# The first stage's silu by tanh, and softplus logarithms for two chunks at a time

## The chip, the cores and the metric

The kernel runs on one core of one Trainium2 chip. The metric is the device time of one execution in microseconds (us). Five engines work side by side, each through a queue of its own in order: PE (matmul, with its weight loads PEld), DVE (vector), ACT (activation functions), POOL (GpSimd) and SP, which here issues most DMAs. [...]

## The reference

The program takes `x` of 8 sequences x 512 positions x 256 channels, in fp32, through two blocks. The change touches the first alone. There, `xn = layernorm(x)` goes into a state-space branch and an FP4 feed-forward branch, and both are added to `x`:

```python
# state-space branch (d_inner 512, d_state 16)
x_in, z = split(xn @ W_in.T)                # 512 channels each
u = silu(causal_conv4(x_in, conv_w) + conv_b)
delta_raw, B, C = split(u @ W_xproj.T)      # 16, 16, 16
delta = softplus(delta_raw @ W_dt.T + b_dt)
h[t] = exp(delta[t] * A) * h[t-1] + (delta[t] * u[t]) * B[t]     # A = -exp(A_log), 512 x 16 states
y[t] = sum_n h[t] * C[t] + D_param * u[t]
attn = (y * silu(z)) @ W_out.T
# feed-forward branch (inner 704); fq: quantize to FP4 in blocks of 16 and back
ffn = fq(silu(fq(xn) @ fq(w_gate).T) * (fq(xn) @ fq(w_up).T)) @ fq(w_down).T
x = x + attn + ffn
```

The second block (block-sparse attention and a two-layer local-attention network) follows on the result, and is the same in both kernels.

## The kernel before, in words

The first stage keeps one sequence of 512 positions at a time on chip, channels on the 128 partitions. Three generators per sequence `b` write its work:

- `head(b)`: layernorm, transposes (`xt`), then for each of four chunks of 128 channels the input projection (`ps_in`), the convolution on DVE (L268, L272), and Silu on ACT into `u` (L275). Then `ps_xp`, and per chunk softplus: `ps_dt` on PE (L294), Abs and Relu (L297, L298), Exp (L299), two DVE operations (L300, L301), Ln (L302), three POOL operations (L303 to L305) that leave `delta` and `du` = delta x u. Softplus is computed as relu(v) + log(1 + exp(-|v|)), and the two DVE operations carry the rounding error of 1 + e.
- `scan(b)`: for two chunks at a time and each of 16 states, `bb` (B spread over the partitions, PE, L366), the product with `du` on DVE (L369), `da` = exp(delta x A) on ACT into PSUM (L374), the scan on DVE (L376), the product with C on POOL (L377), and the sum over states on PE (`y`, L378). After each pair of chunks: `ps_z` (L384), Silu into `z` (L389), the D term on DVE (L390) and the product with `z` on POOL (L393). At the end `ps_o` (L399), the sum into `xs` (L403), and a DMA of the result from ACT's queue (L404).
- `ffn(b)`: FP4 of `xn`, then for four tiles of 128 positions, in two halves of 352 columns: gate and up matmuls (`ps_g` L330, `ps_u` L336), Silu into `h` (L340), the product with up on DVE (L341); FP4 of `h`, transposes and `ps_d` (L350). `fp4` works on DVE (L96 to L100), POOL (L101), ACT (L105), DVE (L106 to L108) and POOL (L109).

`fp4_weights` does the same to the three FFN weights once. `evac` copies from PSUM, in turn on DVE (L50) and ACT (L52).

`beside(scan(b), chain(ffn(b), head(b + 1)), 34, 24)` (36 for the first sequence) interleaves the generators by counts of their `yield`s: while the scan's 34 steps go by, 24 steps of the others are written. A scheduler of the framework then orders each engine's queue from this program, so the order on an engine can differ from the text; it also puts in the table loads (ACT_TABLE_LOAD) that an ACT operation needs when its function isn't in the active table.

The pool `pmm` (tag "mm") has two PSUM banks, which nearly all matmuls of `head` and `ffn` and `ps_z`, `ps_o` share in turn; `bb` and `da` have two banks each, the two `y` one each. `rot` tiles have three buffers by tag (`cv` and `e` use "t0", `w` and `z` "t1"), `hh` six; `delta`, `du` and `u` have two, one for the sequence being scanned and one for the next.

Of the kernel before, what the change touches and what calls it, by code (L numbers as in the profile page):

```python
# [9 lines left out]
FP = mybir.dt.float32  # L10
BF = mybir.dt.bfloat16
AF = mybir.ActivationFunctionType
ALU = mybir.AluOpType
# [4 lines left out]
P = 128  # L18
NB, L, D = 8, 512, 256
NT = L // P  # L20
KC = D // P
DI, NS, DR = 512, 16, 16
NC = DI // P
# [15 lines left out]
def tile_kernel(ctx: ExitStack, tc: tile.TileContext, a: dict, out: bass.AP):  # L39
# [105 lines left out]
    with ExitStack() as s0:  # L145
# [25 lines left out]
        act.activation(a_neg, a_neg, AF.Exp)  # L171
        dve.tensor_scalar(a_neg, a_neg, -1.0, None, ALU.mult)


        sel = w0.tile([DR + 2 * NS, NS, P], FP, name="sel")
        for n in range(NS):
# [21 lines left out]
        def fp4_weights():  # L198
            for name, dst in (("w_gate", w_g), ("w_up", w_u)):
                src = a[name].rearrange("(j p) d -> p j d", p=FB)  # L200
                for j in range(0, FI // FB, 2):
                    raw = q.tile([P, FI], FP, tag="q_src", name="q_src")[:FB, : 2 * D]
                    act.dma_start(raw.rearrange("p (j d) -> p j d", j=2), src[:, j : j + 2, :])
                    fp4(raw, raw, FB, 2 * D, q, sm)
                    ps = pmm.tile([P, L], FP, tag="mm", name="ps_w")
                    for k in range(KC):
                        for i in range(2):
                            pe.transpose(
                                ps[:, (2 * k + i) * FB : (2 * k + i + 1) * FB],
                                raw[:, i * D + k * P : i * D + (k + 1) * P],  # L210
                                ident[:FB, :FB],
                            )
                    evac(
                        dst[:, :, j * FB : (j + 2) * FB],
                        ps[:, : 4 * FB].rearrange("p (k n) -> p k n", k=KC),
                    )
                    yield
            for r in range(D // P):
                raw = q.tile([P, FI], FP, tag="q_src", name="q_src")
                act.dma_start(raw, a["w_down"][r * P : (r + 1) * P, :])  # L220
                fp4(raw, raw, P, FI, q, sm)
                inner_to_partitions(raw, w_d[:, :, r * P : (r + 1) * P])
                yield
# [27 lines left out]
        def head(b):  # L251
            x = load_x(b)
            xn = w1.tile([P, NT, D], FP, tag="xn", name="xn")
            layernorm(x, xn, sm)
            xt = w1.tile([P, KC, L], FP, tag="xt", name="xt")
            to_channels(xn, xt, pmm, "mm")
            yield


            u = w1.tile([P, NC, L], FP, tag="u", name="u")  # L260
            for c in range(NC):
                ps = pmm.tile([P, L], FP, tag="mm", name="ps_in")
                for k in range(KC):
                    pe.matmul(
                        ps, w_in[:, k, c * P : (c + 1) * P], xt[:, k, :], start=(k == 0), stop=(k == KC - 1)
                    )
                cv = rot.tile([P, L], FP, tag="t0", name="cv")
                dve.tensor_scalar(  # L268
                    cv, ps, conv_w[:, c, 3:4], conv_b[:, c : c + 1], ALU.mult, ALU.add
                )  # L270
                for s in range(1, 4):
                    dve.scalar_tensor_tensor(  # L272
                        cv[:, s:], ps[:, : L - s], conv_w[:, c, 3 - s : 4 - s], cv[:, s:], ALU.mult, ALU.add
                    )
                act.activation(u[:, c, :], cv, AF.Silu)  # L275
                yield
            ps = pmm.tile([P, L], FP, tag="mm", name="ps_xp")
            for c in range(NC):
                pe.matmul(
                    ps[: DR + 2 * NS, :], w_xp[:, c, :], u[:, c, :], start=(c == 0), stop=(c == NC - 1)  # L280
                )
            xd = w1.tile([DR + 2 * NS, L], FP, tag="xd", name="xd")
            act.copy(xd, ps[: DR + 2 * NS, :])
            c_d = dram.tile([NS, L], FP, tag="c_d", name="c_d")
            sp.dma_start(c_d, xd[DR + NS :, :])
            yield

            delta = w1.tile([P, NC, L], FP, tag="delta", name="delta")  # L290
            du = w1.tile([P, NC, L], FP, tag="du", name="du")
            for c in range(NC):
                ps = pmm.tile([P, L], FP, tag="mm", name="ps_dt")
                pe.matmul(ps, w_dt[:, c * P : (c + 1) * P], xd[:DR, :], start=True, stop=True)  # L294
                e = rot.tile([P, L], FP, tag="t0", name="e")
                w = rot.tile([P, L], FP, tag="t1", name="w")
                act.activation(e, ps, AF.Abs, bias=b_dt[:, c : c + 1])  # L297
                act.activation(delta[:, c, :], ps, AF.Relu, bias=b_dt[:, c : c + 1])  # L298
                act.activation(e, e, AF.Exp, scale=-1.0)  # L299
                dve.tensor_scalar(w, e, 1.0, None, ALU.add)  # L300
                dve.scalar_tensor_tensor(e, w, 1.0, e, ALU.subtract, ALU.subtract)  # L301
                act.activation(w, w, AF.Ln)  # L302
                pool.tensor_tensor(w, w, e, ALU.subtract)  # L303
                pool.tensor_tensor(delta[:, c, :], delta[:, c, :], w, ALU.add)
                pool.tensor_tensor(du[:, c, :], delta[:, c, :], u[:, c, :], ALU.mult)  # L305
                yield
            made[b] = x, xn, xt, u, xd, c_d, delta, du

        def ffn(b):

            x, xn = made[b][:2]
            xs = sums[b] = w1.tile([P, NT, D], FP, tag="xs", name="xs")
            xq = one.tile([P, NT, D], FP, tag="xq", name="xq")
            for t in range(0, NT, 2):
                fp4(
                    xn[:, t : t + 2, :].rearrange("p t d -> p (t d)"),
                    xq[:, t : t + 2, :].rearrange("p t d -> p (t d)"),
                    P, 2 * D, q, sm,
                )
                yield  # L320
            xqt = one.tile([P, KC, L], FP, tag="xqt", name="xqt")
            to_channels(xq, xqt, pmm, "mm")
            for t in range(NT):
                h = q.tile([P, FI], FP, tag="q_src", name="h")
                n = FI // 2
                for half in range(2):
                    cols = slice(half * n, (half + 1) * n)
                    pg = pmm.tile([P, L], FP, tag="mm", name="ps_g")
                    for k in range(KC):
                        pe.matmul(  # L330
                            pg[:, :n], xqt[:, k, t * P : (t + 1) * P], w_g[:, k, cols],
                            start=(k == 0), stop=(k == KC - 1),
                        )
                    pu = pmm.tile([P, L], FP, tag="mm", name="ps_u")
                    for k in range(KC):
                        pe.matmul(  # L336
                            pu[:, :n], xqt[:, k, t * P : (t + 1) * P], w_u[:, k, cols],
                            start=(k == 0), stop=(k == KC - 1),
                        )
                    act.activation(h[:, cols], pg[:, :n], AF.Silu)  # L340
                    dve.tensor_tensor(h[:, cols], h[:, cols], pu[:, :n], ALU.mult)  # L341
                yield
                fp4(h, h, P, FI, q, sm)
                yield
                ht = q.tile([P, NI, P], FP, tag="ht", name="ht")
                inner_to_partitions(h, ht)
                ps = pmm.tile([P, L], FP, tag="mm", name="ps_d")
                for c in range(NI):
                    m = min(P, FI - c * P)
                    pe.matmul(  # L350
                        ps[:, :D], ht[:m, c, :], w_d[:m, c, :], start=(c == 0), stop=(c == NI - 1)
                    )
                dve.tensor_tensor(xs[:, t, :], x[:, t, :], ps[:, :D], ALU.add)
                yield

        def scan(b):

            x, xn, xt, u, xd, c_d, delta, du = made[b]
            for c0 in range(0, NC, 2):
# [20 lines left out]
                for i in range(2):  # L380
# [5 lines left out]
                            start=(k == 0), stop=(k == KC - 1),  # L386
                        )
                    z = rot.tile([P, L], FP, tag="t1", name="z")
                    act.activation(z, ps, AF.Silu)  # L389
                    dve.scalar_tensor_tensor(  # L390
                        u[:, c, :], u[:, c, :], d_par[:, c : c + 1], ys[i], ALU.mult, ALU.add
                    )
# [16 lines left out]
        for b in range(NB):  # L409
            rest = [ffn(b)] + ([head(b + 1)] if b + 1 < NB else [])  # L410
            if b == 0:
                rest = [fp4_weights(), *rest, rotary_tables()]
            beside(scan(b), chain(*rest), 34, 24 if b else 36)


    with ExitStack() as s1:
# [608 lines left out]
```

## Time and profile before

| | |
|---|---|
| three runs | 4056.45, 4067.31, 4068.78 us; median 4067.31 |
| the profiled execution | 4060.3 us, span 4058.3 us |
| the first stage's last output leaves (L404) | 1726.5 us after the span's start |
| busy share of the whole span | PE 91%, DVE 65%, ACT 42%, POOL 33% |
| mean granted PE clock | 0.91 of full speed |
| sequences leave the first stage (L404) | 313.4, 520.8, 728.6, 933.7, 1141.6, 1346.3, 1551.6, 1726.5 us |
| ACT_TABLE_LOAD in all | 297: 264 in the first stage, 33 in the second |

The page gives busy time by engine, and the span in 40 slices of 101.5 us with the busy share of each in tenths. A group's line has the source line, engine, operation, tiles and shapes, the count, then busy us and mean ns of one, then the engine's idle time just before it and what ended it. A line of the waits names the instruction that waited, what it waited for, and us in total, times and the longest. In an answer by stretch, each row has the length of the stretch, then each engine's busy time (with its count of rows in the trace).

### The profile page before, as it was taken

Reading aid. Unit: us, or ns where it says so; the run is one execution under the profiler, and the core shown is the slowest. Engines: PE = TensorE matmul, PEld = TensorE weight load, DVE = VectorE, ACT = ScalarE, POOL = GpSimd, SP = SyncE. Lnnn points to the kernel's source line nnn. Section 1 sums busy time; section 2 is a strip of 40 time slices with the busy share of each in tenths; the row PEclk is TensorE's granted clock in tenths of the full one; section 3 lists DMA queues with packets and bytes.
Section 4 is the critical chain, followed back from the end, with each engine's and each line's share of the span. In section 5 each row is a group of like instructions: output and inputs, shape, how many; then the busy total and the mean of one; then the engine's idle time right before and its main releaser. Section 6 shows DMA issues by size and latency. Waiting matters only on the chain.

```text
span 4058.3 us, 41394 instructions
## 1 busy us (share of the span) xinstructions
PE 3690.3 (91%) x14428; PEld 1757.7 (43%) x14444; DVE 2647.0 (65%) x4809; ACT 1724.7 (42%) x3411; POOL 1326.4 (33%) x1059
## 2 busy tenths in 40 slices
PE   5889898898988988989999999999999999999998
PEld 1334343434343434344553554544544445445545
DVE  7877879787978787765654555555455456456444
ACT  3454646455645555433343243244234234333333
POOL 4555556555655555521012012021111101201210
PEclk7788789888988888989999999999989999999999
DMA  2111111111111111120011011011101111100100
GB/s 84 45 39 47 45 47 50 44 47 44 47 47 46 49 39 47 60 88 27 27 53 42 14 56 43 20 45 43 38 27 43 38 40 34 53 27 27 48 27 6
DMA packets 88712, 171.96 MB, mean 42 GB/s; under 512 B 10024, under 2 KB 41768, under 8 KB 88504
## 3 DMA queue, kind: packets, MB, share of 16 engines
q1 hardware_dynamic: 85568, 162.95, 12.5%
q10 hardware_dynamic: 2936, 6.36, 0.4%
q8 instruction: 115, 1.88, 0.2%
q14 instruction: 93, 0.76, 0.1%
HBM read 159.58 MB, written 9.70 MB: 42 GB/s over the span
## 4 chain that ended last, share of the span: by engine, by line
PE 46%; DVE 7%; issue 2%; ACT 2%; POOL 1%; DMA 0%; SPq 0%; POOLq 0%; DVEq 0%; ACTq 0%
PE ps_qkv L707 8%; PE ps_g L877 5%; PE ps_a L877 4%; PE ps_wo L839 3%; PE ps_qk L538 3%; PE ps_y L912 2%; PE ps_w L895 2%; PE ps_st L633 2%; PE lo L811 2%; PE pt_qk L698 2%; PE ps_ls L759 2%; DVE pr L788 2%; PE pt L797 1%; DVE nm L769 1%; PE ps_s L583 1%
## 5 line engine op out<-in xcount | busy, mean ns | idle before, releaser
L377 POOL TENSOR_TENSOR hh<-hh,cb 128x512 f32<-128x512 f32 x512 | 660.3, 1302 | 452.3 <-PE y L378 116.8
L378 PE MATMUL y<-hh,ident 128*128 128x512 f32 x1024 | 640.5, 740 | 126.3 <-POOL hh L377 123.5
L376 DVE TENSOR_TENSOR_SCAN hh<-da,hh 128x512 f32<-128x512 f32 x512 | 604.9, 1206 | 11.2 <-ACT da L374 11.1
L374 ACT ACTIVATE da<-delta,a_neg 128x512 f32<-128x512 f32 x512 | 348.7, 689 | 441.1 <-DVE hh L376 439.6
L378 PEld LDWEIGHTS y<-hh,ident 128*128 128x128 f32 x1024 | 202.5, 223 | 460.1 <-POOL hh L377 341.7
L369 DVE TENSOR_TENSOR hh<-du,bb 128x512 f32<-128x512 f32 x512 | 333.9, 672 | 71.7 <-PE bb L366 63.1
L366 PE MATMUL bb<-xd,sel 48*128 48x512 f32 x512 | 311.0, 710 | 26.6 <-DVE hh L369 26.6
L775 ACT ACTIVATE pr<-ps_ls,nm 128x256 f32<-128x256 f32 (+1 forms) x512 | 221.8, 446 | 174.9 <-DVE nm L769 174.7
L726 POOL TENSOR_TENSOR r<-r,r 128x512 f32<-128x512 f32 x128 | 162.8, 1272 | 355.4 <-DVE r L724 355.4
L884 DVE SCALAR_TENSOR_TENSOR ht<-ps_a,b,gl 128x512 f32<-128x512 f32 x96 | 71.9, 749 | 252.1 <-PE ps_a L877 252.1
L487 POOL MEMSET sa<- 128x1 f32 x16 | 1.6, 102 | 711.9 <-DVE sa L843 384.6
L722 DVE TENSOR_TENSOR r<-ps_qkv,tab 128x512 f32<-128x512 f32 x128 | 87.9, 687 | 222.1 <-ACT sq L721 222.1
L883 ACT ACTIVATE gl<-ps_g,b 128x512 f32<-128x512 f32 x96 | 65.9, 686 | 379.4 <-PE ps_g L877 379.4
L877 PE MATMUL ps_g<-hn,wf 128*128 128x512 f32 (+1 forms) x384 | 207.6, 659 | 20.5 <-issue 20.4
L721 ACT ACTIVATE sq<-ps_qkv 128x512 f32<-128x512 f32 x128 | 76.6, 598 | 272.9 <-PE ps_qkv L707 272.9
L877 PE MATMUL ps_a<-hn,wf 128*128 128x512 f32 (+1 forms) x384 | 191.2, 618 | 0.0
L366 PEld LDWEIGHTS bb<-xd,sel 48*128 48x128 f32 x512 | 89.5, 207 | 234.6 <-DVE hh L369 94.6
L637 ACT ACTIVATE pt_e<-ps_st 128x512 f32<-128x512 f32 (+1 forms) x384 | 172.8, 536 | 14.6 <-PE ps_st L631 13.8
L769 DVE TENSOR_REDUCE nm<-ps_ls 128x2 f32<-128x512 f32 (+1 forms) x256 | 147.4, 617 | 43.4 <-PE ps_ls L759 42.6
L707 PE MATMUL ps_qkv<-wqkv,s 128*128 128x512 f32 x384 | 174.9, 605 | 0.0
L707 PE MATMUL ps_qkv<-wqkv,sf 128*128 128x512 f32 x384 | 173.3, 601 | 0.0
L788 DVE TENSOR_SCALAR pr<-pr,lrs 128x256 f32<-128x256 f32 (+1 forms) x512 | 148.6, 332 | 4.8
(213 smaller groups left out, 6622.1 us busy)
## 6 DMA issues: line engine op xcount, KB each, us to landing
cb<-c_d SPq DMA_DIRECT2D x256, 256.0 KB, 3.1
wqkv<-in_wqkv SPq DMA_DIRECT2D x16, 1536.0 KB, 6.2
wf<-in_wf SPq DMA_DIRECT2D x16, 1364.0 KB, 11.0
wf<-in_wf SPq DMA_DIRECT2D x16, 768.0 KB, 4.7
tab<-tab SPq DMA_DIRECT2D x18, 512.0 KB, 6.9
wo<-in_wo SPq DMA_DIRECT2D x16, 512.0 KB, 3.9
x<-in_x SPq DMA_DIRECT2D x8, 512.0 KB, 4.0
x<-xs ACTq DMA_DIRECT2D x8, 512.0 KB, 2.8
```

Source lines behind the costliest of these rows:

```text
L366: pe.matmul(bb, sel[:, n, :], xd, start=True, stop=True)
L369: dve.tensor_tensor(hs[i], du[:, c0 + i, :], bb, ALU.mult)
L374: act.activation(da, delta[:, c, :], AF.Exp, scale=a_neg[:, c, n : n + 1])
L376: dve.tensor_tensor_scan(hh, da, hh, 0.0, ALU.mult, ALU.add)
L377: pool.tensor_tensor(hh, hh, cb, ALU.mult)
L378: pe.matmul(ys[i], ident, hh, start=(n == 0), stop=(n == NS - 1))
L637: act.activation(pt[:, :n], banks[g][:, :n], AF.Exp)
L707: pe.matmul(ps, shifted(s, k, t * P, P), wqkv[:, k, i * IN : (i + 1) * IN], start=(k == 0), stop=(k == KC - 1),)
L769: dve.tensor_reduce(nm, banks[r][:, : 2 * nk].rearrange("p (g n) -> p g n", g=2), AX.X, ALU.max, negate=True)
L775: act.activation(pr[:, at], banks[r][:, at], AF.Exp, bias=nm[:, i : i + 1], accum_out=rs[:, i : i + 1],)
L788: dve.tensor_scalar(pr[:, at], pr[:, at], rs[:, i : i + 1], None, ALU.mult)
L877: pe.matmul(dst[:m], wf1[:, k, off + c * P : off + c * P + m], hn[:, k, :], start=(k == 0), stop=(k == KC - 1),)
```

## The change

Silu(v) is computed as (1 + tanh(v/2)) v/2. The halves are put into the weights once: `conv_w` and `conv_b`, the `z` half of `w_in` (DVE, at the start), and `w_g` (in the evacuation of the quantized gate weight, which moves from `evac` to ACT, with that of `w_u`). ACT writes tanh, and a new DVE operation forms (tanh + 1) times the halved argument: for `u` from SBUF, for the gate and `z` from the PSUM bank that the matmul wrote.

In softplus, `e` becomes one tile of four chunks with a single buffer, and `du` takes the place of `w`. Chunks go in pairs: both chunks' Abs, Relu, Exp and DVE operations first, then one Ln over both, then the POOL operations of both. A pair of chunks now yields four times where it yielded twice, so `head` has 14 steps, before 10, and `ffn` 14 as before; the last argument of `beside` goes from 24 to 28, and from 36 to 40 for the first sequence.

```diff
+        for t in (conv_w, conv_b, w_in[:, :, DI:]):
+            dve.tensor_scalar(t, t, 0.5, None, ALU.mult)
...
-                    evac(
-                        dst[:, :, j * FB : (j + 2) * FB],
-                        ps[:, : 4 * FB].rearrange("p (k n) -> p k n", k=KC),
+                    act.activation(
+                        dst[:, :, j * FB : (j + 2) * FB], ps[:, : 4 * FB].rearrange("p (k n) -> p k n", k=KC),
+                        AF.Copy, scale=0.5 if dst is w_g else 1.0,
                     )
...
-                act.activation(u[:, c, :], cv, AF.Silu)
+                act.activation(u[:, c, :], cv, AF.Tanh)
+                dve.scalar_tensor_tensor(u[:, c, :], u[:, c, :], 1.0, cv, ALU.add, ALU.mult)
...
-            for c in range(NC):
-                ps = pmm.tile([P, L], FP, tag="mm", name="ps_dt")
-                pe.matmul(ps, w_dt[:, c * P : (c + 1) * P], xd[:DR, :], start=True, stop=True)
-                e = rot.tile([P, L], FP, tag="t0", name="e")
-                w = rot.tile([P, L], FP, tag="t1", name="w")
-                act.activation(e, ps, AF.Abs, bias=b_dt[:, c : c + 1])
-                act.activation(delta[:, c, :], ps, AF.Relu, bias=b_dt[:, c : c + 1])
-                act.activation(e, e, AF.Exp, scale=-1.0)
-                dve.tensor_scalar(w, e, 1.0, None, ALU.add)
-                dve.scalar_tensor_tensor(e, w, 1.0, e, ALU.subtract, ALU.subtract)
-                act.activation(w, w, AF.Ln)
-                pool.tensor_tensor(w, w, e, ALU.subtract)
-                pool.tensor_tensor(delta[:, c, :], delta[:, c, :], w, ALU.add)
-                pool.tensor_tensor(du[:, c, :], delta[:, c, :], u[:, c, :], ALU.mult)
-                yield
+            e = one.tile([P, NC, L], FP, tag="e", name="e")
+            for c0 in range(0, NC, 2):
+                cs = (c0, c0 + 1)
+                for c in cs:
+                    ps = pmm.tile([P, L], FP, tag="mm", name="ps_dt")
+                    pe.matmul(ps, w_dt[:, c * P : (c + 1) * P], xd[:DR, :], start=True, stop=True)
+                    act.activation(e[:, c, :], ps, AF.Abs, bias=b_dt[:, c : c + 1])
+                    act.activation(delta[:, c, :], ps, AF.Relu, bias=b_dt[:, c : c + 1])
+                    act.activation(e[:, c, :], e[:, c, :], AF.Exp, scale=-1.0)
+                    dve.tensor_scalar(du[:, c, :], e[:, c, :], 1.0, None, ALU.add)
+                    dve.scalar_tensor_tensor(
+                        e[:, c, :], du[:, c, :], 1.0, e[:, c, :], ALU.subtract, ALU.subtract
+                    )
+                    yield
+                act.activation(du[:, c0 : c0 + 2, :], du[:, c0 : c0 + 2, :], AF.Ln)
+                for c in cs:
+                    w = du[:, c, :]
+                    pool.tensor_tensor(w, w, e[:, c, :], ALU.subtract)
+                    pool.tensor_tensor(delta[:, c, :], delta[:, c, :], w, ALU.add)
+                    pool.tensor_tensor(w, delta[:, c, :], u[:, c, :], ALU.mult)
+                    yield
...
-                    act.activation(h[:, cols], pg[:, :n], AF.Silu)
+                    act.activation(h[:, cols], pg[:, :n], AF.Tanh)
+                    dve.scalar_tensor_tensor(h[:, cols], h[:, cols], 1.0, pg[:, :n], ALU.add, ALU.mult)
...
-                    act.activation(z, ps, AF.Silu)
+                    act.activation(z, ps, AF.Tanh)
+                    dve.scalar_tensor_tensor(z, z, 1.0, ps, ALU.add, ALU.mult)
...
-            beside(scan(b), chain(*rest), 34, 24 if b else 36)
+            beside(scan(b), chain(*rest), 34, 28 if b else 40)
```

## The prediction

> **What bounds the kernel now.** I read the page's slices first, then busy time by stretch, then the groups of table loads, then the Vector engine's waits. The profiled execution has a span of 4058.3 us inside a time of 4060.3, 7.0 below the median of 4067.3; all sums below are made against 4060.3, and a difference is carried over to the median unchanged. The last output of the first stage leaves at 1726.5 us, so the stage is the first 17 of the 40 slices:
>
> ```profile
> PE   5889898898988988989999999999999999999998
> DVE  7877879787978787765654555555455456456444
> ACT  3454646455645555433343243244234234333333
> POOL 4555556555655555521012012021111101201210
> ```
>
> DVE and PE are both at 7 to 9 tenths in those slices, ACT at 3 to 6. ACT is where the change removes work, DVE is where it adds some. Busy time by stretch, cut where each sequence's result is sent to DRAM (columns: length, then PE, PEld, DVE, ACT, POOL busy, PE clock, DMA share, GB/s), shows the sixth, seventh and eighth of eight:
>
> ```profile
> 1141.60:1346.30 204.70, 181.69 (x420) 76.22 (x419) 163.77 (x229) 107.88 (x142) 115.47 (x91) 0.87 0.15 46
> 1346.30:1551.60 205.30, 180.35 (x424) 76.64 (x423) 168.50 (x226) 115.36 (x148) 118.37 (x92) 0.88 0.17 44
> 1551.60:1726.50 174.90, 158.81 (x379) 67.55 (x377) 132.95 (x177) 78.81 (x103) 93.79 (x75) 0.89 0.18 58
> ```
>
> The last stretch has no `head` of a next sequence beside it. It is 30 us shorter, and DVE is busy 33 us less (133.0 against a mean of 166.1). DVE's idle time is 41, 37 and 42 us, the same, although this stretch holds 21 table loads and the two before it 67, 33.5 each. That is the reading that I lean on: **DVE work passes into the stage's time nearly one for one, and fewer table loads alone don't shrink DVE's idle time.** It isn't clean: PE is busy 22 us less too and is the fuller engine there, so PE and DVE share the bound.
>
> The loads, from the groups of the first stage (line, count, busy us, mean ns, idle before):
>
> ```profile
> L374 ACT ACT_TABLE_LOAD x107 | 137.3, 1283 | 1.9
> L340 ACT ACT_TABLE_LOAD x57 | 73.1, 1283 | 1.0
> L302 ACT ACT_TABLE_LOAD x31 | 39.8, 1283 | 0.5
> ```
>
> With L389 (24), L275 (23), L299 (14), L56 (7) and L105 (1) they are 264, 264 x 1.283 = 339 us. What they cost DVE, from its waits in the stage (us in total, times, longest):
>
> ```profile
> DVE h L341 <- ACT h L340: 80.6, 34, 3.3
> DVE hh L369 <- PE bb L366: 63.1, 48, 4.2
> DVE w L300 <- ACT e L299: 26.4, 15, 6.0
> DVE h L341 <- PE ps_u L336: 22.2, 15, 2.5
> DVE q_m L106 <- ACT q_m L105: 16.7, 16, 3.5
> DVE hh L376 <- ACT da L374: 11.1, 10, 3.5
> ```
>
> With two small rows (4.0 and 0.5) ACT ends 139 us of DVE's waits. That, and not 339, is about what the loads can give back. ACT itself waits 440 us for the scan (`da` L374 for `hh` L376): most loads lie in slack.
>
> [...] the load at 946.68 us is followed by its `da` at 947.98, 1.30 later. [...] the trace agrees that Abs and Relu (L297, L298) load nothing, and has no tanh. [...] here a scalar_tensor_tensor takes 738 ns with a PSUM input (L390, 708 to 749) and 959 without (L301, 658 to 1633)[...].
>
> **The change, part by part.**
>
> *Table loads.* The order of the built program holds 42 loads in this stage: 16 before Ln, 16 back to exp (14 at `da`, 2 at the Exp of `e`), and the square roots with the way back. 222 x 1.283 = 285 us leave ACT. The Tanh that replaces Silu I take at Silu's durations (463 ns at 352, 597 to 630 at 512). Sixteen Ln of 1024 replace 32 of 512: fixed part about 0.2 us by the rows at 352 and 512, so 3 us less. All on ACT, so its worth is only what DVE, PE or POOL regain below.
>
> *New DVE work.* Gate of the FFN: 64 of 128x352 from PSUM, 516 (L341) + 50 for the scalar form (738 against 687 ns) = 0.57 us: 36.5. `z`: 32 at 0.738: 23.6. `u`: 32 with SBUF operands alone, 0.74 to 0.96, taken 0.85: 27.2. Scaling w_in, conv_w, conv_b: about 1.9. Four evacuations of gate and up weights go to ACT: -2.1. Together 87; neighbours overlap by some 0.07 us (two L369 in 1.27), 128 x 0.07 = 9 less: **+78**. The one-off scaling waits for w_in, which lands 6.3 us after 0.7, when DVE still has idle time.
>
> *FFN waits.* Now Silu of half 0 frees the gate's PSUM bank on ACT; after, the new DVE operation frees it, and the "mm" ring has two banks. In 23 of 32 tiles the built order puts gate, up, gate, up next to one another on DVE, so half 1 waits: matmuls 1.45 us (L330 at 1004.11), Tanh 0.46, less the 0.52 of the up product between: 1.4; with 0.3 around it 1.7 a tile, 54 in all, against 104 now (80.6 + 22.2 + 1.4). **-50**; from -85 (PE early) to 0 (PE late). Queued on PE behind the waiting gate matmul are the `y` and `bb` of the scan; POOL's next product and DVE's next L369 wait for them.
>
> *Softplus waits.* `du` <- `e`: no load ahead of Exp, 26 falls to about 10: **-16** (-26 to 0). Its first subtraction on POOL now waits for two chunks; POOL is busy 56% of the stage, and only 8.3 us of DVE's waits were for `du`. With `da`: **-8** (-19 to +10).
>
> *Order.* Between the FP4 scale (L100) and L106, which waits for POOL's 1.38 and ACT's 0.79, the built order now has a median of 1.5 us of other DVE work, before 2.9. Of 58 places 45 are short of 2.5 us, before 28; the shortfall grows from 25 to 59 us. The 25 was measured as 16.7, so **+23** (0 to +40). FP4's transposed copies, likewise: **+5**. The 64 new waits of `z` and `u` for Tanh: 0 to 35, taken **+8**.
>
> *At nothing:* SP's transfers are the same, and the second stage's 33 loads stay. `head` yields 14 times, before 10, so `ffn`'s 14 steps now stand beside half of the scan's 34 steps, before beside 58%, and `head`'s have the rest. The work in sum is the same, and DVE is as full in both halves; -10 to +15, since the FFN's tiles then stand closer and `head`'s work further apart.
>
> Sum: 78 - 50 - 16 - 8 + 23 + 5 + 8 = **+40**: 4060 + 40 = 4100 by the profiled execution, 4107 by the median. Chance 0.57 for this, slower, own range 4080 to 4170.
>
> **Rivals.** *Waits on ACT vanish, and nothing takes their place.* Place: the `h`, `w`, `q_m` and `da` rows. Price: 139 us regained, 78 paid: -61, 4006 by the median. It decides once more than 78 of the 139 stay regained. For it: in the tile at 1004 to 1008 us the second half waits 3.26 us for two loads and a `da`, and with its matmul times kept and the loads left out, that tile's last product would end at about 1006.5 instead of 1008.4. Against: the last stretch, where a third fewer loads left DVE's idle time alone. Chance 0.33, with partial forms of it.
>
> *The two cancel:* regain within 12 us (0.3%, about what a measurement of this kernel can tell from no change) of the price. 4067. Chance 0.10.
>
> *PE takes over.* The gate matmul waits for DVE at the head of PE's queue, and `y` and `bb` stand behind it; the -50 and -8 don't come: 78 - 16 + 23 + 5 + 8 = +98, 4165. For it: `bb` already costs DVE 63 us. Against: PE waits just 1 us for `h` now. Part of the 0.57.
>
> *The change doesn't do what it says:* loads might have remained through interleaving. The built order, 42 against 264, leaves little of that.
>
> **Numbers.** Likeliest 4107. The range runs from 3998, just past the rival of 4006, to 4170, past PE's 4165. Faster 0.33, within 0.3% 0.10, slower 0.57.
>
> **What would show it.** Right: ACT busy some 285 us less in the first stage, DVE about 80 us more, DVE's idle time there (now some 320 us to 1700 us) less by no more than 60, the wait of L106 for `q_m` grown, and DVE's row for the new gate operation led by ACT's Tanh behind ps_g. Wrong: DVE's idle time down by more than 80, or its waits on ACT below 40 us; or a stage that shortens while DVE's busy share rises past 85%.

## The result, and the profile after

The changed kernel takes 4109.91 us (median of 4 runs, 4109.13 to 4121.67) against 4068.05 for the kernel before (4 runs, 4056.45 to 4071.02): a ratio of 1.0115, 95% interval 1.0088 to 1.0142. It is slower by 42 us between the medians, and by 47 by the ratio, which isn't the quotient of the two medians (that would be 1.0103). The profiled execution took 4110.3 us, with a span of 4108.5, 50.2 more than before. The first stage ends at 1780.4 us, 53.9 later than before, so all of it was lost there: the second stage takes 2328.1 us, before 2331.8.

The page's slices of the changed kernel, in the same order as before:

```profile
PE   5888888888888888899999999999999999999998
DVE  7888979797978787765645654555455455456444
ACT  3242424243333324323433343243244234333333
POOL 4555645555464646530120121011011111201210
```

ACT fell from 3 to 6 tenths to 2 to 4. DVE has four slices at 9 in the stage, before two. Busy time by stretch for the same three sequences (length, then PE, PEld, DVE, ACT, POOL busy with row counts, PE clock, DMA share, GB/s):

```profile
1172.30:1387.40 215.10, 183.97 (x426) 77.48 (x425) 179.61 (x252) 75.35 (x115) 118.56 (x92) 0.87 0.14 44
1387.40:1602.40 215.00, 183.13 (x427) 77.81 (x426) 178.59 (x242) 75.05 (x115) 119.45 (x94) 0.88 0.15 42
1602.40:1780.40 178.00, 158.60 (x382) 68.67 (x380) 140.59 (x192) 53.06 (x84) 96.93 (x77) 0.91 0.19 58
```

In the first two of these, a sequence takes 10 us more, DVE is busy 10 to 16 us more in it, ACT 33 to 40 us less. Over the whole first stage, from the same view: DVE busy 1398.8 to 1472.1 us (+73), ACT 904.1 to 616.9 (-287), PE 1500.2 to 1488.4; DVE's idle time 327.7 to 308.3 (-19). Together +54, the stage's loss.

The groups of the first stage, table loads first (count, busy us, mean ns, idle before), then the new DVE operations:

```profile
L311 ACT ACT_TABLE_LOAD x16 | 20.5, 1283 | 0.3
L386 ACT ACT_TABLE_LOAD x14 | 18.0, 1283 | 0.2
...
L352 DVE SCALAR_TENSOR_TENSOR h<-h,ps_g 128x352 f32<-128x352 f32 x64 | 32.6, 510 | 39.7 <-ACT h L351 39.5
L279 DVE SCALAR_TENSOR_TENSOR u<-u,cv 128x512 f32<-128x512 f32 x32 | 27.1, 848 | 0.0
L402 DVE SCALAR_TENSOR_TENSOR z<-z,ps_z 128x512 f32<-128x512 f32 x32 | 21.0, 657 | 0.5 <-ACT z L401 0.5
```

The loads did go, 264 to 42. The new gate product (L352) waits 39.7 us for ACT's Tanh. DVE's waits in the stage (us in total, times, longest):

```profile
DVE ht L50 <- PE ps_i L194: 57.2, 30, 2.3
DVE u L403 <- PE y L390: 54.8, 17, 7.6
DVE hh L381 <- PE bb L378: 47.0, 42, 4.6
DVE h L352 <- ACT h L351: 39.5, 32, 1.9
DVE q_m L106 <- ACT q_m L105: 30.2, 31, 2.3
```

Before, the first two rows were:

```profile
DVE ht L50 <- PE ps_i L191: 25.5, 20, 3.5
DVE u L390 <- PE y L378: 13.6, 14, 2.6
```

The wait of the D term (L390, now L403) for `y` is new as a large one: 54.8 us in all and up to 7.6 at a time, before 13.6 and 2.6. POOL's timeline around such a wait shows why (start us, length, engine, line, operation; in brackets the idle time before it):

```profile
933.63 2.50 POOL L314 TENSOR_TENSOR du<-du,e 128x512 f32<-128x512 f32 x2 [1.21 <-ACT du L311]
936.09 1.26 POOL L315 TENSOR_TENSOR delta<-delta,du 128x512 f32<-128x512 f32 x1
937.31 2.49 POOL L389 TENSOR_TENSOR hh<-hh,cb 128x512 f32<-128x512 f32 x2
939.75 1.26 POOL L316 TENSOR_TENSOR du<-delta,u 128x512 f32<-128x512 f32 x1
940.98 1.26 POOL L315 TENSOR_TENSOR delta<-delta,du 128x512 f32<-128x512 f32 x1
942.32 1.26 POOL L316 TENSOR_TENSOR du<-delta,u 128x512 f32<-128x512 f32 x1
943.53 2.49 POOL L389 TENSOR_TENSOR hh<-hh,cb 128x512 f32<-128x512 f32 x2
```

and DVE's in the same microseconds:

```profile
938.73 0.66 DVE L402 SCALAR_TENSOR_TENSOR z<-z,ps_z 128x512 f32<-128x512 f32 x1
946.96 0.75 DVE L403 SCALAR_TENSOR_TENSOR u<-u,d_par,y 128x512 f32<-128x512 f32 x1 [7.57 <-PE y L390]
```

One Ln over two chunks releases six POOL operations of 1.26 us (7.5 us) at once. They fall at the end of a sequence's scan, among the last products with C (L389) in POOL's queue: here three of the six, 3.8 us, stand directly ahead of the last two products. The sum `y` on PE needs those products, DVE's L403 needs `y`, and DVE starts nothing else for 7.57 us. POOL is busy only 55% of the stage (976.5 of 1780.4 us), and still stands last in the chain that ends this wait.

### The profile page after: what moved, and what is told of

The parts are those of the page before. It is cut to its first block, busy times and chain, and to the rows that moved or that the text cites. A ratio compares the mean times of both kernels' runs of the same rounds, so it can differ in the third digit from the quotient of the medians.

```text
span 4108.5 us, 41282 instructions
## 1 busy us (share of the span) xinstructions
PE 3671.2 (89%) x14428; PEld 1755.3 (43%) x14444; DVE 2719.8 (66%) x4936; ACT 1438.6 (35%) x3177; POOL 1330.3 (32%) x1059
## 4 chain that ended last, share of the span: by engine, by line
PE 46%; DVE 8%; issue 2%; ACT 2%; POOL 1%; DMA 0%; SPq 0%; POOLq 0%; DVEq 0%; ACTq 0%
PE ps_qkv L720 8%; PE ps_g L890 5%; PE ps_a L890 4%; PE ps_wo L852 3%; PE ps_qk L551 3%; PE ps_y L925 2%; PE ps_w L908 2%; PE ps_st L646 2%; PE lo L824 2%; PE ps_ls L772 2%; PE pt_qk L711 2%; DVE pr L801 2%; DVE nm L782 1%; PE pt L810 1%; PE o L631 1%
## 5 line engine op out<-in xcount | busy, mean ns | idle before, releaser
L389 POOL TENSOR_TENSOR hh<-hh,cb 128x512 f32<-128x512 f32 x512 | 670.0, 1323 | 521.2 <-PE bb L378 149.5
L390 PE MATMUL y<-hh,ident 128*128 128x512 f32 x1024 | 639.7, 740 | 166.3 <-POOL hh L389 161.4
L390 PEld LDWEIGHTS y<-hh,ident 128*128 128x128 f32 x1024 | 201.1, 222 | 494.3 <-POOL hh L389 392.6
L378 PE MATMUL bb<-xd,sel 48*128 48x512 f32 x512 | 298.8, 684 | 56.6 <-DVE hh L381 56.6
```

What stands on the lines that cost most here:

```text
L378: pe.matmul(bb, sel[:, n, :], xd, start=True, stop=True)
L389: pool.tensor_tensor(hh, hh, cb, ALU.mult)
L390: pe.matmul(ys[i], ident, hh, start=(n == 0), stop=(n == NS - 1))
```

## The experiments

The kernel before ran beside each (its medians were 4061.5 to 4068.1 us). In the table, the median is that of 4 to 20 executions, and the ratio is to the kernel before, with its 95% interval; "steps" is the last argument of `beside` (after the first sequence): more steps put the next sequence's `head` earlier beside the scan. Stage end, PE busy, DVE busy and DVE idle are of the first stage, in us, from the busy time by stretch; the last column is the wait of the D term for `y`. These are from one profiled execution each: that of spare_products_before (4124.04 us) was the slowest of its five, that of tanh_gate_only_36 (4022.27) the fastest of its five.

| kernel | steps | median us | ratio | stage end | PE busy | DVE busy | DVE idle | for `y` |
|---|---|---|---|---|---|---|---|---|
| before | 24 | 4068.05 | 1 | 1726.5 | 1500.2 | 1398.8 | 327.7 | 13.6 |
| after | 28 | 4109.91 | 1.0115 | 1780.4 | 1488.4 | 1472.1 | 308.3 | 54.8 |
| tanh_alone | 24 | 4094.76 | 1.0076 (1.0049 to 1.0102) | 1760.2 | 1484.6 | 1476.7 | 283.4 | 12.6 |
| ln_pairs_alone | 28 | 4048.92 | 0.9966 (0.9955 to 0.9978) | 1722.0 | 1481.9 | 1388.7 | 333.3 | 38.7 |
| no_new_products | 28 | 4065.67 | 1.0002 (0.9992 to 1.0013) | 1736.4 | 1490.1 | 1388.3 | 348.1 | 50.1 |
| head_earlier | 32 | 4045.77 | 0.9946 (0.9929 to 0.9964) | 1708.5 | 1455.9 | 1452.9 | 255.5 | 7.6 |
| before_head_earlier | 27 | 4055.87 | 0.9981 (0.9970 to 0.9992) | 1720.0 | 1487.6 | 1412.6 | 307.4 | 26.5 |
| ln_pairs_head_earlier | 32 | 4066.04 | 1.0008 (0.9989 to 1.0027) | 1746.7 | 1521.3 | 1392.4 | 354.3 | 8.9 |
| head_earlier_36 | 36 | 4032.67 | 0.9922 (0.9897 to 0.9946) | 1705.3 | 1452.0 | 1455.5 | 249.9 | 21.5 |
| no_products_head_earlier | 32 | 4062.10 | 1.0003 (0.9982 to 1.0023) | 1727.5 | 1484.2 | 1381.9 | 345.5 | 23.3 |
| spare_products_before | 24 | 4100.11 | 1.0103 (1.0066 to 1.0139) | 1784.2 | 1548.8 | 1460.0 | 324.1 | 33.3 |
| tanh_gate_only | 28 | 4079.18 | 1.0042 (1.0030 to 1.0054) | 1743.9 | 1473.7 | 1407.0 | 336.8 | 39.4 |
| tanh_gate_only_36 | 36 | 4037.05 | 0.9929 (0.9901 to 0.9956) | 1700.0 | 1452.2 | 1411.5 | 288.4 | 11.7 |
| before_31 | 31 | 4042.56 | 0.9943 (0.9921 to 0.9965) | 1709.5 | 1484.7 | 1392.6 | 316.9 | 10.9 |

In every trace the stage has the same 3436 matmuls, yet PE is busy for 1452.0 to 1548.8 us with them. One and the same matmul can take twice as long: in the kernel before, those of L264 took 592 to 1222 ns. DVE's busy time also moves with the order alone, by 14 us in before_head_earlier and by 19 in head_earlier. So a difference of busy time isn't only work added or taken out.

The first four runs set two theories against each other: that the new DVE work passes into the stage's time, and that the burst on POOL at the end of a sequence does the harm.

**tanh_alone.** The tanh forms with their halves; softplus and steps as before.

```diff
+        for t in (conv_w, conv_b, w_in[:, :, DI:]):
+            dve.tensor_scalar(t, t, 0.5, None, ALU.mult)
...
-                    act.activation(h[:, cols], pg[:, :n], AF.Silu)
+                    act.activation(h[:, cols], pg[:, :n], AF.Tanh)
+                    dve.scalar_tensor_tensor(h[:, cols], h[:, cols], 1.0, pg[:, :n], ALU.add, ALU.mult)
```

(likewise for `u`, `z` and the two evacuations.)

> The tanh forms with their new DVE operations and halved weights, but softplus chunk by chunk and 24 (36) steps, as before the change. Theory 1 (DVE's new work is the whole price, 73 us of busy time in the first stage): some 4110 us or more, since all of that work is here and some 28 table loads come back. Theory 2 (a good part of the price is POOL's burst of six softplus operations per pair of chunks, which lands just before the last state products of a sequence and makes DVE wait for y at the boundary, 54.8 us in the changed kernel against 13.6): the wait of the D term for y falls back to 15 to 25 us, and the time to 4065 to 4085.

Between the two. The ratio says +31 us. DVE is busy 78 us more, and its idle time gave 44 back. With the softplus of before the row in question is as small as before:

```profile
DVE u L397 <- PE y L384: 12.6, 12, 2.6
```

So the tanh forms don't make the boundary wait. Net of what the loads gave back (70 are left of 264), they cost less than half of their DVE work.

**ln_pairs_alone.** Softplus in pairs as in the change, of which the diff shows the Ln alone, and the 28 steps; Silu everywhere.

```diff
-                act.activation(w, w, AF.Ln)
+                act.activation(du[:, c0 : c0 + 2, :], du[:, c0 : c0 + 2, :], AF.Ln)
...
-            beside(scan(b), chain(*rest), 34, 24 if b else 36)
+            beside(scan(b), chain(*rest), 34, 28 if b else 40)
```

> The pairing of the Ln and its 28 (40) steps alone; Silu as before the change, no new DVE work. Theory 1 (DVE work is the price): 4050 to 4068 us, as fast as before or faster, since table loads go and DVE gets nothing to do. Theory 2 (POOL's burst at the boundary is a price of its own): 4085 to 4110, with the wait of the D term for y at 40 us or more.

It is faster than before by 0.34%, and the wait is there all the same:

```profile
DVE u L396 <- PE y L384: 38.7, 23, 5.8
```

So pairing, with the steps that go with it, brings the boundary wait (13.6 to 38.7), and that wait alone doesn't decide the sign. The parts don't add: +31 and -14 by the ratios make +17, and together they cost +47.

**no_new_products.** The kernel after without the three new DVE products (so `u`, the gate and `z` are bare tanh).

```diff
-                dve.scalar_tensor_tensor(u[:, c, :], u[:, c, :], 1.0, cv, ALU.add, ALU.mult)
...
-                    dve.scalar_tensor_tensor(h[:, cols], h[:, cols], 1.0, pg[:, :n], ALU.add, ALU.mult)
...
-                    dve.scalar_tensor_tensor(z, z, 1.0, ps, ALU.add, ALU.mult)
```

> The changed kernel without the three new DVE operations: u, gate and z are tanh of the halved argument alone, so this part of the silu is left out. Table loads and the order of the program's steps as in the change. Theory 1 (each us of DVE work passes into the time): some 4035 us, 75 less than the changed kernel, and below the kernel before. Theory 2 (the burst at the boundary): the same fall by 40 to 75 us, but the wait for y stays at 40 us or more. If the time stays above 4080, DVE's work is not what costs.

84 us of DVE's busy time less moved the stage's end by 44 us and the median by 44. The other 40 came back as idle time. That is Theory 2's fall, with the wait for `y` at 50.1 us; the 75 of Theory 1 didn't come. Its DVE waits:

```profile
DVE h L351 <- PE ps_u L346: 63.3, 39, 2.2
DVE q_m L106 <- ACT q_m L105: 53.8, 38, 2.3
DVE u L400 <- PE y L388: 50.1, 19, 7.0
```

PE now ends the wait for `h`, which in the kernel after it hardly did (L353 for `ps_u`, 5.3 us). With 217 loads fewer than before (47 are left), and without the products that replace Silu, the time is that of before. What the loads gave back went to other waits: against the kernel before, `y` has 37 us more, `q_m` 37, and the products of the gate with `ps_u` 41.

**head_earlier.** The kernel after, with the same operations, `head` four steps earlier. (The order leaves 47 table loads, in the kernel after 42.)

```diff
-            beside(scan(b), chain(*rest), 34, 28 if b else 40)
+            beside(scan(b), chain(*rest), 34, 32 if b else 40)
```

> The changed kernel with 32 in place of 28 as the count of steps beside the scan from the second sequence on: the other strands are written about an eighth earlier, so that head's last softplus pair ends some four states before the sequence's last product. All instructions are the same. Theory 1 (DVE work): 4105 to 4115 us, no change. Theory 2 (burst at the boundary): the wait of the D term for y falls from 54.8 to under 20 us, and the time to 4065 to 4080.

The burst theory has the direction right, and the gain is larger than it said: 64 us by the medians. Its DVE waits:

```profile
DVE hh L381 <- PE bb L378: 44.3, 37, 3.2
...
DVE h L352 <- ACT h L351: 26.5, 22, 1.4
...
DVE u L403 <- PE y L390: 7.6, 6, 3.6
```

The wait for `y` is down by 47 us, that of `h` by 13, that of `ht` by 20. But the stage ends 72 us earlier, and PE is busy 32 us less with the same matmuls, DVE 19 less with the same operations: the steps changed more than the boundary. This is the clearest single result: the change in its place is slower than before by 1.15%, and four steps on, faster by 0.54%.

The next four asked what is left: whether the steps alone do it in any kernel, and which engine bounds once the burst is out of the way.

**before_head_earlier.** The kernel before, with 27 for 24.

```diff
-            beside(scan(b), chain(*rest), 34, 24 if b else 36)
+            beside(scan(b), chain(*rest), 34, 27 if b else 36)
```

> The kernel before with 27 in place of 24 steps beside the scan from the second sequence on, the same shift in proportion as 32 for 28; the instructions are those of before. Theory A (the late end of head costs only where POOL's softplus comes in a burst of six at the boundary): the D term waits for y only 13.6 us in the kernel before, so at most 15 us are to be had, 4050 to 4070. Theory B (an earlier head is worth its 64 us in any kernel): 4000 to 4015.

0.19% faster, in the range of Theory A, but not by its mechanism: the wait for `y` grew from 13.6 to 26.5 us, and that for `bb` fell from 63.1 to 27.4. The same shift is worth 8 us here and 69 by the ratios in the changed kernel.

**ln_pairs_head_earlier.** ln_pairs_alone with 32 for 28, the edit of head_earlier.

> The pairing of the Ln alone, Silu as before the change, with 32 in place of 28 steps. Theory A (the burst at the boundary is a price of the pairing): its wait of the D term for y, 38.7 us, goes to about 10, and the time from 4049 to some 4010 to 4025. Theory B (the 64 us came from something that only the tanh forms have): 4040 to 4055.

Outside both ranges: 17 us slower than ln_pairs_alone, not faster. The wait for `y` fell as Theory A had it (8.9), but no gain came. DVE's idle time rose from 333 to 354 us; the largest rises are in waits that PE ended, such as `xqt` for its transposes (0 to 17.4) and the product with `du` for `y` (0.4 to 21.2), while `bb` stayed (82.5 to 79.2). PE is busy 39 us more with the same matmuls, and the mean granted PE clock in the stage is 0.84, against 0.87. An earlier `head` isn't good in itself, and the boundary wait isn't the whole of the matter.

**head_earlier_36.** The kernel after with 36 for 28.

> The changed kernel with 36 steps, four more than the 32 that gave 4045.8 us. Theory A (only the boundary counts, and at 32 its wait is already 7.6 us): 4040 to 4050, no further gain. Theory B (the earlier the other strands, the better): below 4030. A third way: the FFN's tiles crowd in the first half of the scan and the last steps run bare, then above 4060.

Between A and B, and the fastest median of all: 4032.67, ratio 0.9922. It beats both kernels. Its wait for `y` is longer than with 32 steps (21.5 us, there 7.6), so the boundary isn't what gives this last gain. The granted clock in its stage is 0.89, the highest seen here.

**no_products_head_earlier.** head_earlier without the three products, the edit of no_new_products.

> The changed kernel with 32 steps and without the three new DVE operations, so the factor (1 + tanh), or its halved argument, of the three silus is left out as before. Against 4045.8 us with them, at the same steps. Theory A (DVE's 73 us of new work pass into the time one for one once the boundary is clear): 3960 to 3980. Theory B (they pass at the rate of 0.6 that the pair with 28 steps showed, 44 of 73): 3995 to 4005. Theory C (PE is the bound now): 4030 or more.

In the range of Theory C. (The rate in Theory B's text should be 0.5, 44 of 84.) With DVE busy 71 us **less**, it is **slower** than head_earlier, by 16 us between the medians and 23 by the ratios. PE is busy 28 us more, with the same matmuls. Its DVE waits:

```profile
DVE hh L379 <- PE bb L376: 71.8, 30, 6.1
DVE q_m L106 <- ACT q_m L105: 58.3, 26, 2.3
DVE h L351 <- PE ps_u L346: 54.7, 26, 2.6
```

DVE reaches the `bb` and `ps_u` of PE earlier and waits for them: 126 us in the rows of `bb` and `ps_u`, where head_earlier has 44 for `bb` and 2.4 for `ps_u`. That PE bounds the stage there fits; why its matmuls took longer isn't shown.

The last four priced DVE work in the kernel before, asked whether a smaller form of the change is better, and moved the steps of the kernel before as far as those of the changed one.

**spare_products_before.** The kernel before with Silu kept, and the same 128 DVE operations into a tile that nothing reads.

```diff
                 act.activation(u[:, c, :], cv, AF.Silu)
+                dve.scalar_tensor_tensor(spare, u[:, c, :], 1.0, cv, ALU.add, ALU.mult)
...
                     act.activation(h[:, cols], pg[:, :n], AF.Silu)
+                    dve.scalar_tensor_tensor(spare[:, :n], h[:, cols], 1.0, pg[:, :n], ALU.add, ALU.mult)
...
                     act.activation(z, ps, AF.Silu)
+                    dve.scalar_tensor_tensor(spare, z, 1.0, ps, ALU.add, ALU.mult)
```

> The kernel before, Silu kept, with the same 128 DVE operations beside each Silu, on the same operands, written to a spare tile that nothing reads; they also hold the gate's and z's PSUM bank as the change does. So DVE's price and the bank's without any gain of tables. Theory 1 (DVE's new work passes one for one): 4135 to 4145 us. Theory 2 (at about half, as the changed kernel without the products showed, 44 of 84): 4095 to 4110. Theory 3 (the stage's length is set by PE and its clock, and DVE's work lies beside it): 4060 to 4085.

DVE is busy 61 us more (the new rows alone hold 77), and the median is 39 above that of the kernel before: in Theory 2's range, between a half and two thirds of the work. It isn't a clean price: the profiled execution is the slowest of the five, PE is busy 49 us more in it with the same matmuls, and the wait for `y` is 33.3 us without any pairing. The wait for Silu moved whole to the new operation, with the loads still in it:

```profile
DVE spare L344 <- ACT h L343: 77.2, 37, 2.9
```

The row is 39.5 in the kernel after (L352 for `h`): without the loads this wait is half as long, as the prediction had it.

**tanh_gate_only.** The kernel after with Silu for `u` and `z` (and their weights not halved, which the diff leaves out), so 64 of the 128 products.

```diff
-                act.activation(u[:, c, :], cv, AF.Tanh)
-                dve.scalar_tensor_tensor(u[:, c, :], u[:, c, :], 1.0, cv, ALU.add, ALU.mult)
+                act.activation(u[:, c, :], cv, AF.Silu)
...
-                    act.activation(z, ps, AF.Tanh)
-                    dve.scalar_tensor_tensor(z, z, 1.0, ps, ALU.add, ALU.mult)
+                    act.activation(z, ps, AF.Silu)
```

> Tanh for the FFN's gate alone and the pairing of the Ln with 28 steps; u and z stay on Silu, so 64 of the new DVE operations stay (33 us) and 64 go (48 us), and some 70 of the 222 table loads come back. Theory 1 (DVE's work one for one): 4060 to 4075. Theory 2 (half of it): 4080 to 4095. Theory 3 (PE's clock and the boundary set it): anywhere from 4040 to 4110, with the length of one sequence near a multiple of 3.41 us.

4079.18, in the gap between the first two ranges, and in the wide one of Theory 3: a sequence takes 208.0 to 208.8 us, near 61 x 3.413 = 208.2 (3.413 us is the shortest stretch in the clock record of the kernels before and after; the last section has it). DVE's busy time is 65 us below that of the kernel after, for 31 us; `bb` costs 84.2 us and `y` 39.4.

**tanh_gate_only_36.** The same with 36 steps.

> The same with 36 steps. If the DVE operations of u and z are a price and the boundary is clear at 36, it is faster than the whole change with 36 steps (4032.7): 3995 to 4020. If table loads at the u and z places are the larger price, or PE's clock sets the time, it is not: 4030 to 4060.

4037.05, the same as head_earlier_36 within the intervals, with DVE busy 44 us less. Once more DVE work saved bought nothing at more than 28 steps. Which of the two reasons of the expectation holds isn't settled by it.

**before_31.** The kernel before with 31 for 24.

> The kernel before with 31 steps in place of 24, in proportion what 36 is to 28. If the steps alone are worth as much as in the changed kernel (77 us), 3990 to 4000. If they only undo what the pairing did at the boundary, 4050 to 4070. The kernel with 27 gave 4055.9.

4042.56, between the two. Steps alone are worth 0.57% in the kernel before. At its best setting that ran, the changed kernel is 0.2% better than the kernel before at its own (0.9922 against 0.9943), and the intervals overlap.

## Why the prediction came out right, step by step

The forecast was 4107 and slower; it is 4110. That it is so near is luck in part. The sum of +40 was made on profiled executions, where the change is +50, and +54 at the stage's end; between the medians it is +42. And the sum has to be read term by term, because errors in it nearly cancel.

- **Table loads: right.** 264 to 42, of which 2 stand before a Tanh (L278, L401; none at L351), and ACT's busy time fell by 287 us where 285 were worked out. "Its worth is only what DVE, PE or POOL regain": right too.
- **New DVE work, +78: right, +73.** Gate 510 ns for 570 taken, `z` 657 for 738, `u` 848 for 850; the new rows make 80.7 us. L307 takes 1140 ns where L301 took 959; why isn't shown (it is 958 in ln_pairs_alone, and 1190 in spare_products_before, which has no pairing).
- **FFN waits, -50: right, -57.** 104.2 to 47.4 (39.7 before L352, 7.7 before L353). The 0.3 us around the Tanh was the author's estimate; at 972.24 us of the kernel after, Tanh waited 0.28 for `ps_g`. The rival of PE taking over did not come in the form in which it was put: `bb` costs DVE 47.0 us now, before 63.1, and the -50 came.
- **Softplus waits, -16 and -8: right in size, and incomplete.** `e` 26.4 to 10.1; `da` and `du` 19.4 to 2.7, -17. The failed sentence is "Its first subtraction on POOL now waits for two chunks; POOL is busy 56% of the stage". It asked what waits for `du`, found 8.3 us, and stopped. It didn't ask what stands **behind** the six operations in POOL's queue once they come at once. That is the last product with C, then `y`, then L403: 13.6 to 54.8, **+41, a term missing from the sum.** The burst isn't the only thing that lengthens this wait: before_head_earlier and spare_products_before have 26.5 and 33.3 us without it.
- **Order, +23 and +5.** `q_m` grew by 13.5; the transposed copies by 28 (25.5 + 4 to 57.2 + 0.7), so that term was undersized by 23. (tanh_alone has 47.7 in the first of these rows and ln_pairs_alone 38.7, so both parts of the change bring some; why isn't shown.) Of the +8 for `z` and `u` behind their Tanh, 0.5 came.
- **At nothing: the 24 to 28 steps, -10 to +15.** This was the most sensitive part of the change: another four steps are worth 64 us. What the first four did by themselves stays open, since no run has the pairing with 24.

With the waits as measured: 73 - 57 - 16 - 17 + 13.5 + 28 + 0.5 + 41 - 16 (`bb`) + 7 (`xs` behind `ps_o`) = 57, against 54 for the stage. The prediction came to +40 since the missing 41 and the undersized copies were set off by `bb`, `da`, `q_m`, `z`, the FFN waits and the new work, on each of which it was too pessimistic.

The reading it leaned on, that "DVE work passes into the stage's time nearly one for one", **does not hold in general**. Of DVE's busy time, 84 us less than in the kernel after gives 44; 61 more in the kernel before costs 39; 71 less at 32 steps costs 16. Its second half, that fewer loads alone don't shrink DVE's idle time, agrees with no_new_products: 217 loads fewer than before, and 20 us more idle. The first half was read off the last stretch, in which `head` is missing for PE (22 us) and POOL as well; the prediction named PE's part and then set it aside. The experiments show that the loss goes when the new products go (no_new_products) and also when they stay and the order changes (head_earlier), and that DVE waits for PE instead where its own work is taken out. How the bound is divided among PE, its clock and DVE at each setting, they don't show.

The rival of the vanishing waits (4006) was wrong in the kernel as it stands, but its place was real. DVE's waits that ACT ended did fall, from 139 to 82 us; what took their place were waits for PE and the new work.

## What to carry to other kernels

Loads on an engine with slack are worth only the waits that they end: here 285 us of ACT's work left, and the time rose. When operations are gathered to share a table load, look at the queue into which the gathered results are released, at the end of a loop body above all, and ask what stands behind them there; an engine that is 55% busy can still be the last to arrive. And set the interleaving anew after such a change, in both kernels, before judging it: here four steps weighed more than the change itself, in the changed kernel, and three only 8 us in the kernel before.

## What the runs showed of the hardware

In several kernels the time of one sequence in the first stage keeps to a whole multiple of one length. The trace's record of the granted PE clock switches between 1.0 and 0.5 of full speed, in 212 stretches in the kernel before and 206 in the kernel after; but for the last of each trace, all of them last 3.413 us or a multiple of it, to within 1 ns. From one result's DMA on ACT's queue to the next:

| kernel | us per sequence, the third to the sixth | in 3.413 us |
|---|---|---|
| after | 214.5, 214.9, 215.1, 215.0 | 63 from the fourth on |
| no_new_products | 208.2, 208.2, 208.2, 208.2 | 61 |
| no_products_head_earlier | 208.2, 208.1, 208.2, 208.2 | 61 |
| ln_pairs_head_earlier | 208.3, 211.7, 211.6, 211.6 | 62 from the fourth on |
| head_earlier_36 | 203.4, 204.8, 204.8, 204.8 | 60 from the fourth on |
| spare_products_before | 214.9, 211.4, 211.5, 215.0 | 63, 62, 62, 63 |
| head_earlier | 201.3, 202.4, 203.7, 204.3 | varies |
| before | 207.9, 205.1, 207.9, 204.6 | varies |
| tanh_alone | 212.8, 211.6, 210.1, 209.7 | varies |
| tanh_gate_only_36 | 191.3, 218.8, 190.8, 213.6 | varies |

ACT's timeline has these DMAs (start, length, queue and line). First no_new_products:

```profile
938.53 0.33 ACTq L414 DMA_DIRECT2D x<-xs  x1
...
1146.74 0.33 ACTq L414 DMA_DIRECT2D x<-xs  x1
```

and head_earlier_36:

```profile
923.33 0.33 ACTq L417 DMA_DIRECT2D x<-xs  x1
...
1128.16 0.33 ACTq L417 DMA_DIRECT2D x<-xs  x1
```

The periods are 208.21 and 204.83 us; 61 and 60 times 3.413 are 208.2 and 204.8. In the kernel after the clock record itself repeats: stretches at half speed begin at 909.3, 940.0, 984.4 and 1011.7 us, and again at 1124.3, 1155.1, 1199.4 and 1226.7, each 215.0 later. Cut into lengths of 3.413 us, 99% of the record from 520 to 1560 us is as it was 63 lengths before; in the kernel before, no shift of 50 to 74 lengths gives more than 73%. Between the kernel after and no_new_products 10.5 us of DVE's busy time per sequence (84 / 8) went, and the period fell by 6.8 us, two such lengths. The steps alone, 28 and 32, went with another granted clock in the stage (0.87 in ln_pairs_alone, 0.84 in ln_pairs_head_earlier) and with another period (205.1 to 208.0 us from the third sequence to the sixth, there 208.3 to 211.7). Whether the clock sets the period, and whether that is why the parts don't add up, wasn't tested.
